# A layer of graph attention and routed low-rank feed-forward: the first pair of items on an uncentred W, with x centred instead

## The chip, the core and the metric

The program runs on one core of a Trainium2 chip. The core has five engines, each with its own queue of instructions carried out in order: TensorE (PE, matrix products), VectorE (DVE), ScalarE (ACT), GpSimd (POOL) and SyncE (SP, which here only issues transfers). They wait for each other through semaphores. Sixteen DMA engines move data between memory (HBM) and the core's SBUF; PE writes its results into PSUM. The metric is the time of one execution on the device in microseconds (us); less is better.

## The reference

The input x is 128 items of 128 rows by 1024 columns, adj a 128 x 128 matrix of 0 and 1 for each item. For each item:

```python
h  = layernorm(x)                       # over the 1024 columns, eps 1e-5
Wh = (h @ W) as 16 heads of 64          # W is 1024 x 1024
e  = leaky_relu(Wh . a1 + Wh . a2)      # one score per row and head
att = softmax(where(adj == 0, -9e15, e)) * adj
x1 = x + elu(att @ Wh)
n  = layernorm(x1)
gates = softmax of the top 2 of n[0] @ router.T   # 8 experts
x2 = x1 + n + sum over experts: gate * (n @ down.T) @ up
```

The score of a row does not depend on the column of adj, so softmax has two values per row. Two facts matter for the change. The mean that layernorm subtracts can be taken off x, or, since the same number is subtracted from a whole row of x, off the columns of W: (x - mean(x)) @ W = x @ (W - column mean of W) = (x - mean(x)) @ (W - column mean of W). And the score a . (x @ W) can be had from extra columns W . a ("score columns") that go through the same product.

## The kernel before

**Tiling.** Items are taken in pairs (q = 0 to 63), and pairs in groups of two (four items, g). For each pair the product with W is made by a Strassen-like scheme: x and W are cut into 2 x 2 blocks and seven block products take the place of eight. `pair_sums` (L245) makes the sums of the transposed x on POOL. `project` (L274) issues the seven products, `product_1` to `product_7`, each 8 fp32 matmuls (16 records in the trace) of 128 rows by 260 columns: 256 columns of W (`MAIN`) and 4 score columns (`SCORES`). W stands in SBUF as seven blocks of `w_sb`: B11, B21, B22, and the combinations T1, T2, T3, NT4; T1 first holds B12.

**Order.** The scheduler is off: each engine carries out its instructions in the order in which the code issues them. The loop at L692 has eight gaps for each pair; what stands in gap n is issued before the n-th product step. So the lists `gaps[...]` are the order of the work on every engine. In a pair's gaps stand: attention weights of the pair before (`attention_weights`, L368), `attend` and `update` of its two items, `second_stats`, `turn` (a 16-bit copy on ACT and a transposing DMA), `rejoin`, `join`, `high` and `low` (L358, L362: the product split into two parts for the attention matmuls), and the statistics (`first_stats`) and sums of the next pair. In the second pair of a group also `fetch`, `ffn_down`, `ffn_up` of the group before.

**Start.** SP and ACT load W in 16 pieces, then x_t of pair 0, adj, router and down matrices. `prepare` (L674) fills the gaps of pair 0. `spread_a` spreads a1 + a2 over the partitions, `column_means` (L153) makes the column means of W with 16 matmuls of 512 columns, `score_products` and `score_columns` (L161 to L179) make the score columns of all W on POOL and DVE, `center_block` (L188) subtracts the means from a block, score columns included, and `combine` (L671) and `weights_3_main` (L663) make the combinations. The block B11 is loaded, scored and centred before product_1 of pair 0.

**Experts.** `experts` (L195) centres the router and down matrices with 16 matmuls and two subtractions and stores the down rows as a table. It is issued ahead of pair 1's products.

Of the kernel before, what the change touches and what calls it, by code (L numbers as in the profile page):

```python
# [8 lines left out]
F32 = mybir.dt.float32  # L9
# [4 lines left out]
AF = mybir.ActivationFunctionType  # L14
# [11 lines left out]
def adj_ffn_kernel(  # L26
# [6 lines left out]
    w: bass.AP,  # L33
    a: bass.AP,
    down_t: bass.AP,
# [76 lines left out]
    a_rows = work.tile([1, 2, D], F32, tag="parts", name="a_rows", bufs=1)  # L112
    nc.sync.dma_start(a_rows, a[None])
    load_x(0)
    for h in range(NH):
        for k in range(KC):
            (nc.scalar, nc.sync)[k % 2].dma_start(
                w_at(h, k)[:, :, MAIN], in_two(w[k * P:(k + 1) * P, h * HALF:(h + 1) * HALF]))
    load_xt(0)
    router_sb = const.tile([P, KC, E], F32, name="router_sb")  # L120
    down_sb = work.tile([P, G * TOP, R, KC], F32, tag="down", name="down_sb", bufs=1)
    load_adj(0)
    nc.scalar.dma_start(router_sb, router_t)
    nc.scalar.dma_start(down_sb, down_t)
# [5 lines left out]
    one_row = const.tile([1, P], F32, name="one_row")  # L130
    nc.vector.memset(one_row, 1.0)
    mean_of = work.tile([P, P], F32, tag="dn", name="mean_of")
    nc.vector.memset(mean_of, 1.0 / D)
    ones_g = const.tile([G, P], F32, name="ones_g")
# [6 lines left out]
    a_sum = work.tile([P, NH, HALF], F32, tag="ex", name="a_sum", bufs=1)  # L141
    w_mean, score_mean = [], []

    def spread_a():

        nc.vector.tensor_add(a_rows[:, 0], a_rows[:, 0], a_rows[:, 1])
        for h in range(NH):
            pa = ps_m.tile([P, HALF], F32, tag="pm", name="pa")
            nc.tensor.matmul(pa, one_row, a_rows[:, 0, h * HALF:(h + 1) * HALF],
                             start=True, stop=True)  # L150
            nc.scalar.copy(a_sum[:, h], pa)

    def column_means(h):  # L153
        pc = ps_m.tile([P, HALF], F32, tag="pm", name="w_mean")
        for k in range(KC):
            nc.tensor.matmul(pc, mean_of, w_at(h, k)[:, :, MAIN], start=(k == 0),
                             stop=(k == KC - 1))
        w_mean.append(in_two(pc))


    def score_products(h):  # L161
        prod = work.tile([P, KC, 2, QC], F32, tag="y_t", name="prod", bufs=1)
        for k in range(KC):
            nc.gpsimd.tensor_tensor(prod[:, k], w_at(h, k)[:, :, MAIN], in_two(a_sum[:, h]),
                                    ALU.mult)
        return prod
# [4 lines left out]
    def score_columns(h, prod):  # L171
        for k in range(KC):
            by_head(w_at(h, k)[:, :, SCORES], prod[:, k])

    def score_columns_at_once(h):
        for k in range(KC):
            prod = work.tile([P, 2, QC], F32, tag="hp", name="prod")
            nc.vector.tensor_mul(prod, w_at(h, k)[:, :, MAIN], in_two(a_sum[:, h]))
            by_head(w_at(h, k)[:, :, SCORES], prod)  # L179

    def score_means(h):
        prod = work.tile([P, 2, QC], F32, tag="hp", name="prod")
        nc.vector.tensor_mul(prod, w_mean[h], in_two(a_sum[:, h]))
        mean = small.tile([P, 2, HPQ], F32, tag="score_mean", name="score_mean", bufs=2)
        by_head(mean, prod)
        score_mean.append(mean)

    def center_block(h, b):  # L188

        for cols, mean in ((MAIN, w_mean[h]), (SCORES, score_mean[h])):  # L190
            part = w_sb[:, b, :, :, cols]
            nc.vector.tensor_tensor(part, part, mean[:, None].to_broadcast(part.shape),
                                    ALU.subtract)

    def experts():  # L195

        pr = ps_m.tile([P, HALF], F32, tag="pm", name="pr")[:, 0:E]
        for k in range(KC):
            nc.tensor.matmul(pr, mean_of, router_sb[:, k], start=(k == 0), stop=(k == KC - 1))
        nc.vector.tensor_tensor(router_sb, router_sb,  # L200
                                pr[:, None].to_broadcast([P, KC, E]), ALU.subtract)
        pc = ps_m.tile([P, E, R], F32, tag="pm", name="pc")
        for k in range(KC):
            nc.tensor.matmul(pc, mean_of, down_sb[:, :, :, k], start=(k == 0), stop=(k == KC - 1))
        nc.vector.tensor_tensor(down_sb, down_sb,
                                pc[:, :, :, None].to_broadcast([P, E, R, KC]), ALU.subtract)
# [16 lines left out]
        return slot, down_row, up_row  # L223
# [50 lines left out]
    def project(q):  # L274
# [11 lines left out]

        def bank():
            return ps_w.tile([P, 2, HALF], F32, tag="pw", name="pw")

        def product(dst, first, lhs, rhs):  # L290
            for j in range(2):
                for k in range(KH):
                    nc.tensor.matmul(dst[:, j, 0:QE], lhs[:, k, :], w_sb[:, rhs, k, j],  # L293
# [6 lines left out]
        def read(dst, src, plus):  # L300
            nc.vector.tensor_tensor(dst, src[:, :, 0:QE], plus, ALU.add)  # L301

        p1, u2, u4 = (temp(n) for n in ("p1", "u2", "u4"))
        banks = {}
# [7 lines left out]
        def product_1():  # L312
            product(*to("x"), a11, B11)
            nc.scalar.copy(p1, banks["x"][:, :, 0:QE])

        def product_2():
            product(*to("x"), a12, B21)
            WH[q, 0] = banks["x"]
            high(q, 0)
# [475 lines left out]
```

## Time and profile before

Columns: what, time in us.

| | us |
|---|---|
| median of four runs | 1966.0 (1965.66 to 1968.01) |
| the profiled execution | 1966.55 |
| its span | 1963.6 |
| PE busy in the span | 1938.4 (99%) |
| DVE / ACT / POOL busy | 1664.7 / 1077.3 / 848.6 |
| first product of pair 0 starts on PE | 29.95 |
| first matmul of the experts | 61.36 |
| first product of pair 1 | 66.84 |
| product_4 of pair 1 | 89.75 |
| first logits (pair 2) | 116.44 |

Span is the time from the first to the last recorded instruction. An engine is busy while it carries out an instruction; waiting for a semaphore is not busy. fp32 matmuls appear as two records each. Gaps on PE are named with what ended them.

### The profile page before, as it was taken

How to read it: one execution, taken by the hardware profiler on the slowest of the kernel's cores; microseconds unless marked ns; L12 is line 12 of the kernel's file. 1: busy time of each engine (PE TensorE's matmuls, PEld its weight loads, DVE VectorE, ACT ScalarE, POOL GpSimd, SP SyncE). 2: the span in 40 equal slices, each digit the busy share in tenths (PEclk: the TensorE clock that was granted, in tenths of full speed). 3: DMA queues.
4: the chain of work that ended last, by engine and by line, in shares of the span. 5: the costliest groups of instructions: out<-in, count | busy, mean ns of one | idle time of the engine just before them, and what ended most of it. 6: DMA issues, size and time to landing. Idle time of an engine off the chain costs nothing.

```text
span 1963.6 us, 30104 instructions
## 1 busy us (share of the span) xinstructions
PE 1938.4 (99%) x11010; PEld 1577.0 (80%) x11010; DVE 1664.7 (85%) x3512; ACT 1077.3 (55%) x1027; POOL 848.6 (43%) x1128
## 2 busy tenths in 40 slices
PE   7999999999999999999999999999999999999997
PEld 4888888888888888888888888888888888888885
DVE  8788888888888888888888888898888898888886
ACT  0365555565555555555555655655655655655653
POOL 4353443553344553344543334544335544435530
PEclk9999999999999999999999999999999999999998
DMA  5356566555555565566565565565566565565552
GB/s 194 110 138 191 168 162 187 150 163 183 163 171 185 143 178 175 157 183 182 135 188 171 154 187 182 127 199 170 151 186 174 137 199 172 151 188 165 147 161 96
DMA packets 346580, 324.98 MB, mean 166 GB/s; under 512 B 274241, under 2 KB 280385, under 8 KB 346433
## 3 DMA queue, kind: packets, MB, share of 16 engines
q1 hardware_dynamic: 326386, 278.45, 48.8%
q0 software_dynamic: 17008, 40.91, 7.2%
q10 hardware_dynamic: 3040, 3.70, 0.6%
q8 instruction: 87, 1.43, 0.3%
q14 instruction: 59, 0.48, 0.1%
HBM read 189.31 MB, written 67.63 MB: 131 GB/s over the span
## 4 chain that ended last, share of the span: by engine, by line
PE 92%; DVE 4%; DMA 2%; ACT 1%; issue 0%; POOL 0%; ACTq 0%; DVEq 0%; POOLq 0%
PE pw L293 78%; PE ph L406 6%; PE pu L595 3%; PE pd L579 3%; PE pb L542 1%; DMA tt<-halves 1%; PE pl L486 1%; DMA w_sb<-in_w 1%; DVE xn L424 1%; DVE xn L425 1%; DVE hp L416 0%; DVE w_sb L169 0%; PE pu L656 0%; ACT halves L456 0%; ACT y_t L462 0%; DVE stats L229 0%
## 5 line engine op out<-in xcount | busy, mean ns | idle before, releaser
L293 PE MATMUL pw<-w_sb,xt 128*128 128x260 f32 x4096 | 947.5, 386 | 2.9 <-DVE parts L364 1.7
L293 PEld LDWEIGHTS pw<-w_sb,xt 128*128 128x128 f32 x4096 | 767.4, 190 | 149.2 <-issue 25.6
L293 PE MATMUL pw<-w_sb,s 128*128 128x260 f32 x3072 | 711.2, 385 | 3.3 <-DVE w_sb L672 2.5
L293 PEld LDWEIGHTS pw<-w_sb,s 128*128 128x128 f32 x3072 | 578.1, 190 | 116.4 <-issue 21.2
L233 POOL TENSOR_SCALAR rstd<-mv 128x2 f32<-128x2 f32 x128 | 29.1, 227 | 868.8 <-DVE mv L230 863.6
L462 ACT COPY y_t<-tt 128x2048 uint16<-128x2048 uint16 x126 | 312.8, 2502 | 67.5 <-DMA tt<-halves 67.3
L229 DVE BATCH_NORM_STATS2 stats<-xn 128x6 f32<-128x512 f32 x512 | 324.0, 675 | 5.4 <-DMA xn<-in_x 5.3
L560 POOL DMA_INDIRECT down<-table,at_down x248 | 251.7, 1015 | 162.3 <-DVE e L380 88.7
L456 ACT COPY halves<-xn 128x2048 uint16<-128x2048 uint16 x126 | 239.3, 1899 | 141.7 <-DVE xn L425 141.7
L360 ACT ACTIVATE parts<-wh,rstd 128x512 fp32r<-128x512 f32 x192 | 134.2, 716 | 235.7 <-DVE wh L301 235.7
L423 ACT ACTIVATE ex<-hp 128x1024 f32<-128x1024 f32 x128 | 135.4, 1058 | 178.8 <-DVE hp L416 178.8
L599 DVE SCALAR_TENSOR_TENSOR xn<-pu,rstd,xn 128x512 f32<-128x512 f32 x248 | 169.0, 744 | 21.8 <-PE pu L595 21.8
L416 DVE TENSOR_TENSOR hp<-ph,att 128x512 f32<-128x512 f32 x256 | 161.4, 672 | 9.9 <-PE ph L406 9.6
L425 DVE SCALAR_TENSOR_TENSOR xn<-ex,xn 128x1024 f32<-128x1024 f32 x128 | 156.9, 1226 | 14.0 <-DVE xn L424 0.9
L406 PE MATMUL ph<-parts,adj_f 128*128 128x512 f32 x512 | 164.3, 442 | 1.3 <-ACT parts L360 0.8
L301 DVE TENSOR_TENSOR wh<-pw,u 128x520 f32<-128x520 f32 x128 | 89.2, 697 | 84.7 <-PE pw L293 81.6
L424 DVE SCALAR_TENSOR_TENSOR xn<-hp,xn 128x1024 f32<-128x1024 f32 x128 | 156.8, 1225 | 4.4
L478 ACT ACTIVATE xn<-xn,off,mul 128x1024 f32<-128x1024 f32 x128 | 151.3, 1231 | 1.6 <-POOL off L443 1.6
L364 DVE SCALAR_TENSOR_TENSOR parts<-wh,rstd,parts 128x512 fp32r<-128x512 f32 x192 | 138.9, 751 | 12.0 <-ACT parts L360 12.0
L301 DVE TENSOR_TENSOR wh<-pw,p 128x520 f32<-128x520 f32 x64 | 44.8, 700 | 80.8 <-PE pw L293 80.8
L406 PEld LDWEIGHTS ph<-parts,adj_f 128*128 128x128 f32 x512 | 96.5, 189 | 20.3 <-ACT parts L360 1.2
L234 POOL TENSOR_TENSOR rstd<-rstd,half_pow 128x2 f32<-128x2 f32 x128 | 91.5, 715 | 10.6
(117 smaller groups left out, 1506.2 us busy)
## 6 DMA issues: line engine op xcount, KB each, us to landing
xn<-in_x SPq DMA_DIRECT2D x128, 512.0 KB, 6.8
xt<-in_x_t SPq DMA_DIRECT2D x128, 512.0 KB, 5.2
out_y<-xn SPq DMA_DIRECT2D x124, 512.0 KB, 3.9
adj_f<-in_adj_t POOLq DMA_DIRECT2D x32, 256.0 KB, 3.1
adj_i<-in_adj SPq DMA_DIRECT2D x32, 256.0 KB, 2.6
down<-table,at_down POOLq DMA_INDIRECT x248, 4.0
w_sb<-in_w ACTq DMA_DIRECT2D x8, 256.0 KB, 6.1
w_sb<-in_w SPq DMA_DIRECT2D x8, 256.0 KB, 5.6
```

Of the source, the lines that this page charges most:

```text
L229: nc.vector.bn_stats(st[:, h, :], X[i][:, h * HALF:(h + 1) * HALF])
L293: nc.tensor.matmul(dst[:, j, 0:QE], lhs[:, k, :], w_sb[:, rhs, k, j], start=(first and k == 0), stop=(k == KH - 1), skip_group_check=not f ...
L364: nc.vector.scalar_tensor_tensor(in_two(PARTS[q][:, 1, b]), block, rstd, in_two(PARTS[q][:, 0, b].bitcast(F32)), op0=ALU.mult, op1=ALU.sub ...
L406: nc.tensor.matmul(PH[i][h], GRP[g]["adj_f"][:, t, :], PARTS[q][:, s, NH * (i % 2) + h], start=(s == 0), stop=(s == 1))
L416: nc.vector.tensor_tensor(hp[:, h * HALF:(h + 1) * HALF].rearrange("p (h f) -> p h f", f=F), ph.rearrange("p (h f) -> p h f", f=F), att[:, ...
L424: nc.vector.scalar_tensor_tensor(xt, hp, 0.0, xt, op0=ALU.max, op1=ALU.add)
L425: nc.vector.scalar_tensor_tensor(xt, ex, 1.0, xt, op0=ALU.min, op1=ALU.add)
L456: nc.scalar.copy(halves, X[i].bitcast(U16).rearrange("p (d s) -> p s d", s=2))
L462: nc.scalar.copy(y_of(i).bitcast(U16).rearrange("p k (n s) -> p s k n", s=2), TT.pop(i).rearrange("p (s k) n -> p s k n", s=2))
L478: nc.scalar.activation(X[i], X[i], AF.Identity, bias=GRP[g]["off"][:, t:t + 1], scale=GRP[g]["mul"][:, t:t + 1])
L560: nc.gpsimd.indirect_dma_start(out=st["down"][:, j * R:(j + 1) * R].rearrange("p r k -> p (r k)"), out_offset=None, in_=table, in_offset=b ...
L599: nc.vector.scalar_tensor_tensor(y[:, cols], pu[t], st["rstd"][:, t:t + 1], y[:, cols], op0=ALU.mult, op1=ALU.add)
```

## The change

The first pair no longer needs a centred W. `center_x` subtracts the row means from the transposed x of pair 0, with means made on PE. product_1 and product_2 then use B11 and B21 as loaded. As product_1 alone covers half of the rows of W, its result p1 is corrected by `correct_p1` before the other products are added to it. B11, B21 and B22 are centred in place later, one after another, and T1, T2, T3 and NT4 are combined from them (T1 is no longer centred by itself).

The column means are made in two steps on PE column tiles: `partial_means` puts the sums of four k chunks into four strips of 32 partitions, and `column_means` adds the strips with one matmul. The score columns no longer come from products on POOL and DVE: a transposed copy of W (`w_t`) is loaded, `score_rows` multiplies it with a on column tiles, `center_rows` subtracts the mean, `turn_rows` transposes, and `score_columns` copies the results into `w_sb`. Pair 0 itself has products of 256 columns; its scores are made from its results by `score_of` (a product on POOL, a sum on DVE).

W is laid out on the host in four contiguous blocks. SP issues all loads: a, x_t, B11, B21, x, B22, T1 (B12), then W_t, adj, the next pair. The router and down matrices are loaded in gap 5 of pair 0, and `experts` now sums over the k chunks on DVE first, so that two matmuls do, and stands in gap 6 of pair 1, between product_3 and product_4. In pair 0, product_7 goes ahead of product_6, and the next pair's statistics and sums move from gaps 3 and 4 to gap 6.

```diff
-    for h in range(NH):
-        for k in range(KC):
-            (nc.scalar, nc.sync)[k % 2].dma_start(
-                w_at(h, k)[:, :, MAIN], in_two(w[k * P:(k + 1) * P, h * HALF:(h + 1) * HALF]))
     load_xt(0)
+    wt_sb = work.tile([P, KH, D], F32, tag="y_t", name="wt_sb", bufs=1)
+    wt_at = [wt_sb[:, c] for c in range(KH)]
+    wt_at += [work.tile([P, D], F32, tag="x", name="wt", bufs=10) for _ in range(KH)]
+    for i, b in enumerate((B11, B21, B22, T1)):
+        if i == 2:
+            load_x(0)
+        nc.sync.dma_start(w_sb[:, b], w[:, i])
+    nc.sync.dma_start(wt_sb, w_t[:, 0:KH])
+    for c in range(KH, KC):
+        nc.sync.dma_start(wt_at[c], w_t[:, c])
...
+    def center_x():
+        xt = XT[0]
+        px = ps_m.tile([P, HALF], F32, tag="pm", name="px")[:, 0:2 * P]
+        mean = px.rearrange("p (t n) -> p t n", t=2)
+        for k in range(KC):
+            nc.tensor.matmul(mean, mean_of, xt[:, :, k], start=(k == 0), stop=(k == KC - 1))
+        for t, lo, hi in ((0, 0, KH), (0, KH, KC), (1, 0, KC)):
+            part = xt[:, t, lo:hi]
+            nc.vector.tensor_tensor(part, part, mean[:, t, None].to_broadcast(part.shape),
+                                    ALU.subtract)
+
+    def partial_means(h):
+        pc = ps_m.tile([P, HALF], F32, tag="pm", name="pc")
+        for u in range(2):
+            for c in range(KH):
+                nc.tensor.matmul(pc[c * 32:(c + 1) * 32], mean_of[:, 0:32],
+                                 w_sb[:, BLOCK[h][u], c, :, MAIN], start=(u == 0), stop=(u == 1),
+                                 tile_position=(0, c * 32))
+        part = work.tile([P, HALF], F32, tag="hp", name="part")
+        nc.scalar.copy(part, pc)
+        return part
+
+    def column_means(part):
         pc = ps_m.tile([P, HALF], F32, tag="pm", name="w_mean")
-        for k in range(KC):
-            nc.tensor.matmul(pc, mean_of, w_at(h, k)[:, :, MAIN], start=(k == 0),
-                             stop=(k == KC - 1))
+        nc.tensor.matmul(pc, sum_of, part, start=True, stop=True)
         w_mean.append(in_two(pc))
...
+    def score_rows():
+        rows = [ps_m.tile([P, HALF], F32, tag="pm", name="rows") for _ in range(NH)]
+        for half in range(2):
+            for n in range(NH):
+                for t in range(KH):
+                    c = half * KH + t
+                    nc.tensor.matmul(rows[n][t * 32:(t + 1) * 32], a_two[:, c],
+                                     wt_at[c][:, n * HALF:(n + 1) * HALF],
+                                     start=(half == 0), stop=(half == 1),
+                                     tile_position=(0, t * 32))
+        return rows
+
+    def center_rows(rows):
+        sums = small.tile([P, NH], F32, tag="sums", name="sums", bufs=1)
+        for n in range(NH):
+            nc.vector.tensor_reduce(sums[:, n:n + 1], rows[n], AX.X, ALU.add)
...
+        for n in range(NH):
+            nc.scalar.activation(turned[:, n], rows[n], AF.Identity, bias=less)
+        return turned
+
+    def turn_rows(turned):
...
+            for k in range(KH):
+                nc.tensor.transpose(pt[:, k], turned[:, u, k * P:(k + 1) * P], ident)
...
+    def score_columns(cols):
...
+        for h, u, dst in ((0, 0, of[B11]), (0, 1, of[B21]), (1, 1, of[B22]), (1, 0, b12)):
+            src = cols[u].rearrange("p k (j t r) -> p k j t r", j=2, t=2)
+            for j in range(2):
+                nc.vector.tensor_copy(dst[:, :, j].rearrange("p k (t f) -> p k t f", t=2),
+                                      src[:, :, j, :, 2 * h:2 * h + 2])
+        nc.vector.tensor_tensor(of[T3], of[B22], b12, ALU.subtract)
+        for dst, x, y, op in ((T2, T3, B11, ALU.add), (T1, B22, T2, ALU.subtract),
+                              (NT4, B21, T2, ALU.subtract)):
+            nc.vector.tensor_tensor(of[dst], of[x], of[y], op)
+
+    def score_of(b):
...
+        nc.gpsimd.tensor_tensor(prod, src, a_sum[:, h], ALU.mult)
+        by_head(dst, prod)
...
     def experts():
-        pr = ps_m.tile([P, HALF], F32, tag="pm", name="pr")[:, 0:E]
-        for k in range(KC):
-            nc.tensor.matmul(pr, mean_of, router_sb[:, k], start=(k == 0), stop=(k == KC - 1))
...
+        for t, n in ((router_sb.rearrange("p k e -> p e k"), E), (down_rows, ER)):
+            sums = work.tile([P, ER], F32, tag="hp", name="sums")
+            nc.vector.tensor_reduce(sums[:, 0:n], t, AX.X, ALU.add)
+            pr = ps_m.tile([P, HALF], F32, tag="pm", name="pr")[:, 0:n]
+            nc.tensor.matmul(pr, mean_of, sums[:, 0:n], start=True, stop=True)
+            nc.vector.tensor_tensor(t, t, pr[:, :, None].to_broadcast([P, n, KC]), ALU.subtract)
...
+        gaps[0] += [(place_a,), (spread_a,), (center_x,), (pair_sums, 0)]
+        gaps[2] += [keep("part 0", partial_means, 0), (first_stats, 0),
+                    keep("less", first_half), (first_stats, 1),
+                    keep("", column_means, "part 0"), (keep_c11,), (high, 0, 0),
+                    (combine, T3, B22, T1, ALU.subtract)]
+        gaps[3] += [keep("part 1", partial_means, 1), (center_block, 0, B11),
+                    keep("", correct_p1, "less"), (combine, T2, T3, B11, ALU.add), (center_block, 0, B21)]
+        gaps[4] += [keep("", column_means, "part 1"), keep("rows", score_rows), (score_of, 0),
+                    (center_block, 1, B22), (combine, T1, B22, T2, ALU.subtract),
+                    keep("turned", center_rows, "rows")]
+        gaps[5] += [(combine, NT4, B21, T2, ALU.subtract), (load_experts,)]
+        gaps[6] += [keep("cols", turn_rows, "turned"), (score_of, 3)]
+        gaps[7] += [keep("", score_columns, "cols"), (score_of, 1)]
...
-            gaps[3].append((first_stats, 2 * q + 2))
-            gaps[4] += [(pair_sums, q + 1), (first_stats, 2 * q + 3)]
+            gaps[3 if q else 6].append((first_stats, 2 * q + 2))
+            gaps[4 if q else 6] += [(pair_sums, q + 1), (first_stats, 2 * q + 3)]
...
+        if q == 0:
+            gaps[7].append((score_of, 2))
         if q == 1:
-            slot, down_row, up_row = experts()
+            gaps[6].append((experts,))
```

## The prediction

> **What bounds the kernel now.** I read the engines' shares first, then the busy time by stretches, then the timeline of the first 120 us, the chain that ended last, and the groups of the operations that the change uses anew.
>
> ```profile
> PE 1938.4 (99%) x11010; PEld 1577.0 (80%) x11010; DVE 1664.7 (85%) x3512; ACT 1077.3 (55%) x1027; POOL 848.6 (43%) x1128
> 120.00:1900.00 1780.00, 1779.73 (x10278) 1458.15 (x10277) 1521.11 (x3254) 1013.43 (x963) 785.85 (x1050) 1.00 0.58 169
> ```
>
> The second line is a stretch: its length, then busy time of PE, its weight loads, DVE, ACT, POOL. From 120 us on PE is busy 1779.73 of 1780 us, and the change touches nothing there. So it is worth what it does to the moment at which PE reaches a fixed point of this stream; I take the last product of pair 1 (product_4), 89.75 us before.
>
> ```profile
> 29.95 3.77 PE L293 MATMUL pw<-w_sb,xt 128*128 128x260 f32 x16 [0.52 <-DVE w_sb L192]
> 40.70 3.77 PE L293 MATMUL pw<-w_sb,s 128*128 128x260 f32 x16 [2.52 <-DVE w_sb L672]
> 61.36 1.85 PE L199 MATMUL pr<-router_sb,mean_of 128*128 128x8 f32 x16
> 63.06 3.96 PE L204 MATMUL pc<-down_sb,mean_of 128*128 128x128 f32 x16
> 66.84 3.69 PE L293 MATMUL pw<-w_sb,xt 128*128 128x260 f32 x16
> 71.45 0.19 DVE L397 TENSOR_TENSOR att<-p,den 128x32 f32<-128x32 f32 x1
> ...
> 86.25 3.67 PE L293 MATMUL pw<-w_sb,s 128*128 128x260 f32 x16
> 89.75 7.18 PE L293 MATMUL pw<-w_sb,xt 128*128 128x260 f32 x32
> 92.42 1.32 ACT L360 ACTIVATE parts<-wh,rstd 128x512 fp32r<-128x512 f32 x2
> 93.16 1.42 DVE L364 SCALAR_TENSOR_TENSOR parts<-wh,rstd,parts 128x512 fp32r<-128x512 f32 x2 [2.50 <-ACT parts L360]
> ```
>
> Columns: start, length, engine, operation. Pair 0's products begin at 29.95, after W has been loaded, its score columns made and B11 centred; the experts' 32 matmul records hold PE from 61.36 to 66.84; pair 1 begins there. The last two lines matter most: pair 1's two low halves end at 94.57 (93.16 + 1.42), 4.8 us after product_3 of that pair left PE. No matmul before pair 1's attention waits for them now.
>
> ```profile
> 71.75 1.30 DVE hp L416 x2
> ...
> 81.50 1.91 ACT halves L456
> 83.43 4.31 DMA tt<-halves
> ...
> 90.15 2.36 ACT xn L478 x2
> 92.51 0.62 ACT parts L360
> 93.16 1.42 DVE parts L364 x2
> ```
>
> That is the chain (start, length) from attention's end at 71.64 to the lows: two updates on DVE, the 16-bit copy, the transposing DMA, rejoin, two joins, the highs. 22.93 us, of which PE sets nothing.
>
> **Gain in the head, step by step** (a sum of rows of the trace; columns per second of PE from rows: 16 records of 260 columns follow each other every 3.505 us, so 256 columns 3.45 us and 512 columns 0.43 us a record; 0.27 us more until the result is out, 3.77 less 3.50).
>
> Removed from ahead of the first product: on DVE eight score products and reduces (means 1.00 and 0.68 us), the score means and B11's centring, which fill 12.17 to 29.9; on PE 32 w_mean records; later the second reduces (4.8) and all centring of T1. SP takes over what ACT issued (10 transfers, some 0.5 us an issue, all gone out ahead of the data, which is 0.37 MB per us whatever the queue).
>
> x_t now goes first. In the trace 1.03 MB had moved by 5.42 us and then 0.37 MB per us; x_t and adj_f are 1.3 MB, so x_t is there at 6.5. Until 18.3 us PE ran at half pace (0.86 us between w_mean records, 0.43 after; 5.1 us after the 13.81 restart). center_x has 16 records of 256 columns: 12 at 0.43, 4 at 0.22, ending 12.7 with the drain. Bounds: full pace by 8 us, 1.5 earlier; half pace throughout, 1.2 later.
>
> Subtract 0.68, product_1 3.45 + 0.27, copy of p1 0.59, product_2 3.45: PE at 21.1. The loads of B11 and B21 (2.1 MB) are in by 12.5, so they hide. partial_means runs 16 records on four column tiles. The nearest row is the down product:
>
> ```profile
> L579 PE MATMUL pd<-y_t,down x1984: 272/273/328, 137.6 to 1915.7; 128*32 128x128 f32 x199
> 196.78 1.98 PE L579 MATMUL pd<-y_t,down 128*32 128x128 f32 x64
> ```
>
> 64 records of 128 columns in 1.9 us, 0.030 each: four tiles at once, so 0.119 for 512 columns and 1.9 us for sixteen. PE at 23.0, result 23.2; ACT copy 0.59; sum matmul 0.86; product_7 24.8 to 28.2, second partial_means to 30.1. T3 (DVE, 2.28) needs the last block of W: 6.4 MB, 19.5 us plus a landing, about 21; done 23.5, hidden under the DVE wait below.
>
> DVE: low of block 0 waits in order for its high (ACT: part copy, c11 copy 0.59, high 0.72, so 25.1) and ends 25.9; center B11 2.27, the p1 correction 0.75 (a 512-column row of this form), T2 2.28: 31.1; center B21 33.3. product_6 waits for T2 and starts 31.1, issues to 34.6; second sum matmul; score_rows 32 records, 3.8, to 39.3 (W_t, 4 MB more, is in by 33). DVE: u2 0.7 after product_6, a reduce 0.69, center B22, T1: 40.7. product_5 waits for it: 40.7 to 44.2. u4 0.7; product_3 45.2 to 48.6; eight transposes (the tail's 16 records took 2.1) 1.9; product_4 to 54.0, NT4 long ready at 48.1.
>
> Then PE waits. Pair 1's product_1 reads score columns that DVE writes in program order after: wh0 (50.1); score 3's reduce, whose product stands on POOL behind three mask operations (0.7) and adj_f's issue (0.68), so 52.2 and 52.9; two statistics 3.1; two lows 1.5; wh1 0.7; two copies. That is 58.2, against 66.84. The queue behind score 3's reduce is thus the price: some 4.2 us of PE. SP keeps up: its loads of x for pair 1 land by 38, and the experts' two loads are moved behind them and have 45 us.
>
> So pair 1 begins 8.6 us earlier. Of these 5.5 are the experts' matmuls, only moved; the pair itself ends 3 us earlier.
>
> **What is given back.** The experts now stand between product_3 and product_4 of pair 1. In PE's order the first matmul waits for a DVE reduce that stands behind the two lows. Attention of pair 0 ends late: POOL has pair 1's sums (rows of 5.24 together), rstd 0.94, and two score products 1.28 each, to 61.0; reduce 0.69; the 2.7 us from e to att: 64.4. Add the 22.93 of the chain: lows end 87.3. Reduce 0.22, matmul 0.48, the router subtraction 0.22, reduce of the down rows 1.22, second matmul: PE is free for product_4 at 89.8. product_3 had ended at 82.1 (58.2 + 22.9, and 1.0 for a DVE that runs 1.5 later against PE than before). PE thus waits 5.7 + 1.7 us there. Against 89.75: +0.1 us. Bounds from the chain: if the copy and rejoin rows vary as they do between pairs, 1.5 either way.
>
> **Pace of PE after the waits.** Ends: after 2.52 us of idle (before 40.70) the records kept their 381 ns, so 0; after 4.12 us (before 13.81) PE ran at half pace for 5.1 us, 2.55 lost, though it had not been at full pace ahead of that. I take 0 for the 4.2 us wait, since DVE and not PE sets what follows (0.7 at most), and for 5.7 + 1.7 a slow stretch that counts from the experts' first matmul, 2.0 us ahead of product_4: 3.1 us at half pace, 1.55 lost. Sum: 0.1 + 1.55 = +1.7.
>
> [...]
>
> The profiled run took 1966.55 us (span 1963.6 and 2.95 around it), 0.55 above the median of four, 1966.0. +1.7 makes 1968.3 for it, and **1967.7** for a median.
>
> **Rivals.**
> 1. Faster: the gain is kept. Place: the experts' wait in pair 1. If the chain from attention to the lows is shorter there than 22.93, or DVE reaches the experts' reduces soon after product_3 (wh0 0.7, highs and lows 1.5 to 3, then the two-matmul sequence 2.2), PE waits some 4.5 instead of 7.4 us and keeps its pace: 1962. For it speaks only that PE comes earlier; against it that ACT and the transposing DMA, not PE, end last in that chain.
> 2. Slower: the column tiles take turns. Place: 64 new records. At 0.43 us each instead of 0.119, the first partial_means costs 5.0 more, the second 4.0 (1.0 was waiting), score_rows 8.6 (1.4 was waiting): +17.6, 1985. It decides (crossing +3.9) from about 0.19 us a record. Against it stands the pd row, with four moving operands and weights reloaded as here.
> 3. Slower by pace: center_x at half pace throughout (+1.2), both waits followed by a slow stretch (+0.7 and 2.55): 0.1 + 4.5 = 1970.6. For it: the 13.81 row. Against: the first wait ends near the 4.12 us that is the shortest evidence.
> 4. It does not do what it says: a load of W or W_t is late. W_t has 6 us of cover under product_6, T1 2; beyond that each us costs one. Not likely at 0.37 MB per us.
>
> **How the numbers follow.** About 0.2%, 3.9 us, is what a measurement of this kernel can tell from no change. Forecast (head gain handed back, within 3.9): 0.60. Pace lost twice, or the chain late as well: 0.19. Tiles in turns or partly so: 0.07. Late load: 0.01. Gain kept: 0.13. Slower is 0.27, same 0.60, faster 0.13. The forecast's own bounds are 0.1 - 1.5 - 1.5 = 1963.1 and 0.1 + 1.5 + 1.2 + 2.55 + 0.7 = 1972; taking in the upper part of the faster rival, the range is 1962 to 1973.
>
> **What would show it.** Right: pair 1's first 260-column product near 58 us behind a wait of some 4 us for DVE; score_rows and partial_means at about 0.12 us a record; the experts' two matmuls near 88 and 89.5 with 5 to 6 and 1.7 us of idle before them, released by DVE reduces; product_4 of pair 1 within 3 us of 89.75; logits near 118 against 116.44; from there equal. Wrong: no wait at the experts, column-tile records at 0.4 us, or new idle after 120 us.

## The result and the profile after

The changed kernel takes 1970.45 us (median of 40 runs, 1968.76 to 1972.8), the kernel before, run beside it, 1967.35 (60 runs, 1965.16 to 1970.15). The ratio is 1.0016, with a 95% interval of 1.0011 to 1.0020: slower by 0.16%, some 3 us, which is inside the 0.2% that a measurement of this kernel can tell from no change. The four runs of before that were shown ahead of the prediction had a median 1.35 below that of the sixty.

The profiled execution of the changed kernel took 1970.55 us, span 1968.7; that of before 1966.55, 0.8 below its median of sixty. Comparisons of the two profiles so overstate the loss by some 0.9 us. First the engines' shares from the page after:

```profile
PE 1936.6 (98%) x11042; PEld 1576.0 (80%) x11042; DVE 1654.2 (84%) x3511; ACT 1080.8 (55%) x1031; POOL 837.2 (43%) x1123
```

and two stretches of it (length, then busy time of PE, of its weight loads (PEld), DVE, ACT, POOL, then the clock of PE that was granted, 1.00 being full speed, DMA share and GB/s):

```profile
120.00:1900.00 1780.00, 1779.48 (x10290) 1457.79 (x10290) 1520.17 (x3251) 1016.03 (x964) 788.32 (x1056) 1.00 0.58 169
60.00:125.00 65.00, 59.29 (x262) 49.63 (x260) 50.52 (x103) 32.64 (x30) 18.67 (x30) 0.91 0.32 83
```

From 120 us on PE is busy 1779.48 of 1780 us, against 1779.73 before: that part is as it was. Everything happens ahead of it, and in the second stretch (60 to 125 us) PE is idle for 5.7 us and its clock is 0.91. The timeline of PE after shows where (start, length, line, operation, and in brackets the idle time before it and what ended it):

```profile
50.14 3.62 PE L373 MATMUL pw<-w_sb,xt 128*128 128x256 f32 x16
59.34 2.94 PE L373 MATMUL pw<-w_sb,xt 128*128 128x260 f32 x6 [5.58 <-issue]
...
66.89 3.67 PE L373 MATMUL pw<-w_sb,s 128*128 128x260 f32 x16
...
81.84 3.67 PE L373 MATMUL pw<-w_sb,s 128*128 128x260 f32 x16
89.74 0.59 PE L283 MATMUL pr<-sums,mean_of 128*128 128x8 f32 x2 [4.23 <-DVE sums L281]
91.82 0.80 PE L283 MATMUL pr<-sums,mean_of 128*128 128x128 f32 x2 [1.48 <-DVE sums L281]
92.41 9.06 PE L373 MATMUL pw<-w_sb,xt 128*128 128x260 f32 x32
...
120.80 0.55 PE L568 MATMUL pl<-router_sb,y_t 128*4 128x8 f32 x16
```

Pair 0's last product is issued by 53.8, then PE waits 5.58 us. ("issue" means that the profile names no releaser. The products wait for the score columns: DVE's copies of them into `w_sb` start at 59.08.) Pair 1 begins at 59.34, 7.5 us earlier than before (66.84). It starts slowly: 6 records in 2.94 us, at half pace. product_3 of pair 1 starts at 81.84; then the experts' two matmuls wait 4.23 and 1.48 us for sums on DVE. product_4 of pair 1 and product_1 of pair 2, one row of 32 records, start at 92.41, 2.66 us later than before (89.75), and take 9.06 us where they took 7.18. The first logits come at 120.80, against 116.44. The head is 7.5 us shorter, and 60 us later PE is 4.4 us late.

The chain of waits after (start, length) says what carries that from pair 1's start on:

```profile
53.77 5.57 issue
59.34 6.79 PE pw L373 x16
...
76.51 1.91 ACT halves L538
...
78.43 4.26 DMA tt<-halves
...
85.09 2.36 ACT xn L560 x2
87.45 0.62 ACT parts L442
...
88.10 0.65 DVE parts L446
...
89.51 0.19 DVE sums L281
...
89.74 0.61 PE pr L283 x2
...
90.56 1.22 DVE sums L281
...
91.82 0.80 PE pr L283 x2
92.62 8.86 PE pw L373 x32
```

It is the chain shown for before, from the updates over the 16-bit copy, the transposing DMA and the highs to the lows on DVE (88.10 + 1.42 = 89.52), but with a new end: from the lows through the experts' sum, matmul, sum, matmul to product_4. Before, nothing of PE ahead of pair 1's attention hung on the lows. That the slow first product (59.34) stands on this chain does not make it dear: DVE's first update waited only 0.43 us for PE behind it, and experiment 5 puts a number to it.

### The profile page after: what moved, and what is told of

Read it like the earlier page. It is cut to its first block, busy times and chain, and to the rows that moved or that the text cites. A ratio compares the mean times of both kernels' runs of the same rounds, so it can differ in the third digit from the quotient of the medians.

```text
span 1968.7 us, 30167 instructions
## 1 busy us (share of the span) xinstructions
PE 1936.6 (98%) x11042; PEld 1576.0 (80%) x11042; DVE 1654.2 (84%) x3511; ACT 1080.8 (55%) x1031; POOL 837.2 (43%) x1123
## 4 chain that ended last, share of the span: by engine, by line
PE 92%; DVE 3%; DMA 2%; ACT 2%; issue 1%; POOL 0%; SPq 0%; POOLq 0%; DVEq 0%
PE pw L373 77%; PE ph L488 6%; PE pu L677 3%; PE pd L661 3%; DMA tt<-halves 1%; PE pb L624 1%; PE pl L568 1%; ACT y_t L544 1%; ACT halves L538 1%; DVE xn L507 1%; DVE xn L506 1%; DVE stats L306 0%; DVE hp L498 0%; PE pu L738 0%; DMA xt<-in_x_t 0%
## 5 line engine op out<-in xcount | busy, mean ns | idle before, releaser
L373 PE MATMUL pw<-w_sb,xt 128*128 128x260 f32 (+1 forms) x4096 | 952.3, 387 | 7.0 <-issue 5.6
L373 PE MATMUL pw<-w_sb,s 128*128 128x260 f32 (+1 forms) x3072 | 711.1, 385 | 2.9 <-DVE w_sb L746 2.0
L381 DVE TENSOR_TENSOR wh<-pw,u 128x520 f32<-128x520 f32 (+1 forms) x128 | 89.4, 698 | 88.4 <-PE pw L373 84.8
L381 DVE TENSOR_TENSOR wh<-pw,p 128x520 f32<-128x520 f32 (+1 forms) x64 | 44.8, 700 | 81.6 <-PE pw L373 81.6
L311 POOL TENSOR_TENSOR rstd<-rstd,half_pow 128x2 f32<-128x2 f32 x128 | 91.5, 715 | 10.6
```

Source lines behind the costliest of these rows:

```text
L373: nc.tensor.matmul(dst[:, j, cols], lhs[:, k, :], w_sb[:, rhs, k, j, cols], start=(first and k == 0), stop=(k == KH - 1), skip_group_check ...
```

## The experiments

The theory: the head's gain is real, and it is lost because the new `experts` stands between product_3 and product_4 of pair 1, behind the lows on DVE, which follow the end of pair 0's attention and not PE. The rivals: the loss comes from DVE's waits in pair 0 (score 3); it is the half clock after PE's idle times; or the new parts of the head, the column tiles above all, do not pay.

| | pair 1 starts | attention of pair 0 ends | first logits | median us | ratio to before, 95% |
|---|---|---|---|---|---|
| before | 66.84 | 71.64 | 116.44 | 1967.35 | 1 |
| the change | 59.34 | 66.19 | 120.80 | 1970.45 | 1.0016 (1.0011 to 1.0020) |
| experts as before | 59.58 | 68.34 | 114.13 | 1963.09 | 0.9975 (0.9965 to 0.9985) |
| experts' move alone | 62.9 | 67.40 | 121.62 | 1970.47 | 1.0011 (1.0002 to 1.0020) |
| score 3 later | 57.10 | 65.57 | 119.06 | 1969.04 | 1.0005 (0.9996 to 1.0014) |
| experts in two parts | 59.56 | 66.42 | 115.34 | 1965.11 | 0.9985 (0.9976 to 0.9994) |
| PE kept busy | 60.12 | 66.97 | 120.30 | 1969.07 | 1.0007 (0.9998 to 1.0016) |
| means without tiles | 68.72 | 75.58 | 129.98 | 1979.57 | 1.0061 (1.0047 to 1.0075) |
| experts as before, score 3 later | 59.68 | 67.92 | 113.04 | 1962.34 | 0.9976 (0.9965 to 0.9986) |
| lean experts | 58.77 | 65.09 | 114.92 | 1964.77 | 0.9986 (0.9977 to 0.9995) |
| lean experts, index rows first | 58.90 | 65.24 | 110.80 | 1960.16 | 0.9963 (0.9949 to 0.9976) |

The three times in the first columns are from each kernel's own profiled execution (attention's end is the end of the instruction `att`; 62.9 is 16 records after the 59.35 start of a row of 32). Logits and the profiled execution go together: from the logits to the span's end it is 1846 to 1848 us in all of them. Each ratio is to executions of the kernel before taken beside that kernel, whose medians lay between 1967.12 and 1968.26; across the rows the ratios are to be compared rather than the medians.

**1. Put the experts back.** The changed kernel, with the experts of before issued ahead of pair 1's products.

```diff
-            gaps[6].append((experts,))
+            slot, down_row, up_row = experts()   # 16 + 16 records on PE, no sums on DVE
```

> The changed kernel with the experts undone alone: 32 matmul records again, issued ahead of pair 1's products. Theory (the head's gain is handed back at the experts' wait between product_3 and product_4 of pair 1): PE waits 5.6 us before pair 1 in the changed kernel anyway and now spends it on the experts' 5.5 us, so pair 1 still begins near 59.5; product_4 follows product_3 at once, near 83 to 85 instead of 92.4; the logits come near 113 (120.8 in the changed kernel, 116.4 before): 3 us or 0.2% faster than before. Rival (the time is lost in pair 0, in DVE's wait or in the tiles): the logits stay near 120 and the time 3 us above before.

PE's timeline with the experts put back:

```profile
53.81 1.85 PE L277 MATMUL pr<-router_sb,mean_of 128*128 128x8 f32 x16
55.52 3.95 PE L282 MATMUL pc<-down_sb,mean_of 128*128 128x128 f32 x16
59.58 3.75 PE L374 MATMUL pw<-w_sb,xt 128*128 128x260 f32 x16
78.88 5.43 PE L374 MATMUL pw<-w_sb,xt 128*128 128x260 f32 x16 [2.11 <-issue]
87.65 7.18 PE L374 MATMUL pw<-w_sb,xt 128*128 128x260 f32 x32
```

The experts' 32 records fill the 5.6 us in which PE waited anyway, and pair 1 starts at 59.58 all the same: ahead of pair 1 they cost PE nothing in the changed kernel. They do cost DVE: with the subtractions ahead of it, attention of pair 0 ends at 68.34 instead of 66.19. product_4 starts at 87.65, 4.8 us sooner than with the change, and the time falls to 0.9975 of before. So the head's gain is real, and the experts, in place and form together, make the difference between -0.25% and +0.16%; experiment 4 keeps the new form and changes the place. A wait of 2.11 us remains in pair 1 and is followed by a slow product (5.43 instead of 3.67).

**2. The experts' move alone.** The kernel before, with only the new `experts` in gap 6 of pair 1.

```diff
-            slot, down_row, up_row = experts()
+            gaps[6].append((experts,))           # with the new experts()
```

> The kernel before with the new experts alone (DVE sums, two matmuls, between product_3 and product_4 of pair 1), head untouched. Theory: pair 1 begins 5.5 us earlier, near 61.4, but PE waits for the lows; DVE comes to attention some 6 us earlier, near 65.4, the lows end near 88.3, product_4 starts near 91 (89.75 before), and a slow stretch of PE adds up to 2: 1 to 3 us slower than before. Rival (the 32 records were the cost and the wait is hidden): 4 to 5 us faster.

PE's timeline with that move alone:

```profile
82.25 3.67 PE L292 MATMUL pw<-w_sb,s 128*128 128x260 f32 x16
90.83 0.59 PE L205 MATMUL pr<-sums,mean_of 128*128 128x8 f32 x2 [4.91 <-DVE sums L203]
92.91 0.80 PE L205 MATMUL pr<-sums,mean_of 128*128 128x128 f32 x2 [1.49 <-DVE sums L203]
93.50 8.71 PE L292 MATMUL pw<-w_sb,xt 128*128 128x260 f32 x32
```

The same two waits and the same slow stretch, without any of the new head. Pair 1 starts 4 us sooner and the kernel is 0.11% slower (1.0002 to 1.0020): this part of the change by itself gains nothing, and its loss, within the 0.2% of the measurement, is like that of the whole change. Of the 5.5 us that pair 1 should have gained, 1.5 were lost in pair 0 of this execution: the last 6 records of the product that ends at 45.97 took 2.35 us, where 7 took 1.70 before, and the next product starts at 47.70 instead of 46.20, both behind a wait of 1.72 us (see the last section).

**3. Score 3 later.** In the changed kernel the sum of score 3, which stood in DVE's queue ahead of pair 1's statistics and the lows, goes behind the score columns.

```diff
-        gaps[6] += [keep("cols", turn_rows, "turned"), (score_of, 3)]
-        gaps[7] += [keep("", score_columns, "cols"), (score_of, 1)]
+        gaps[6] += [keep("cols", turn_rows, "turned")]
+        gaps[7] += [keep("", score_columns, "cols"), (score_of, 3), (score_of, 1)]
```

> The changed kernel with the third score (POOL product and DVE sum) moved behind the score columns, so that DVE does not wait for it ahead of the statistics. Theory: pair 1 begins 2.5 to 3 us earlier (59.3 to about 56.5), but POOL's products end when they did, attention ends where it did (66.2) and the experts' matmuls and product_4 stay where they are (92.4 within 1): the time is that of the changed kernel, 3 us above before, within 1. Rival (DVE's wait in pair 0 sets the cost): 3 us faster than the changed kernel, level with before.

Pair 1 starts at 57.10, 2.2 us sooner; attention ends 0.6 us sooner, product_4 starts at 91.28 (1.1 sooner) behind waits of 5.26 and 1.49 us, and the time is within 0.1% of before. The expectation was the changed kernel's time within 1 us; by the ratios it is some 2 us better, which is nearer to what the rival said, though the two intervals overlap. The reading of the first wait (DVE behind score 3's sum, which waits for POOL) is right, but an earlier pair 1 mostly makes the experts' wait longer: 5.26 us instead of 4.23, with pair 1 2.2 us sooner and product_4 only 1.1. So score 3's place is at most a part of the loss: the ratio stays 0.3% above that of experiment 1, and with the experts back (experiment 7) moving score 3 changes nothing measurable.

**4. The experts in two parts.** Their two sums stay in gap 6 of pair 1; matmuls, subtractions and the rest go to gap 2 of pair 2.

```diff
-            gaps[6].append((experts,))
+            gaps[6].append((expert_sums,))
+        if q == 2:
+            gaps[2].append((experts,))
```

> The changed kernel with the experts' two DVE sums left in gap 6 of pair 1 and their two matmuls and the rest put into gap 2 of pair 2, where nothing waits. Theory: pair 1 begins near 59.3 as in the changed kernel, product_4 follows product_3 without a wait (near 85.6 instead of 92.4) and at full pace; 1 to 2 us come back as waits for a late DVE; logits near 113 to 114: 2 to 4 us faster than before. Rival (the loss sits in pair 0 or the pace): the time stays above before.

PE's timeline with the experts in two parts:

```profile
80.81 3.67 PE L381 MATMUL pw<-w_sb,s 128*128 128x260 f32 x16
84.32 7.18 PE L381 MATMUL pw<-w_sb,xt 128*128 128x260 f32 x32
...
96.68 0.60 PE L291 MATMUL pr<-sums,mean_of 128*128 128x8 f32 x4
...
106.47 5.43 PE L381 MATMUL pw<-w_sb,xt 128*128 128x260 f32 x16 [2.17 <-issue]
```

product_4 starts at 84.32 directly behind product_3, and the experts' records (96.68) wait for nothing. The head, the sums and the matmuls are those of the change; the place of the matmuls alone brings the ratio from 1.0016 to 0.9985, some 6 us by the ratios. 2 us are missing against the first experiment; a wait of 2.17 us has come up in pair 2 (before 106.47), again with a product of 5.43 us behind it, so that the logits come at 115.34 and not at the expected 113 to 114.

**5. Keep PE busy in the waits.** The changed kernel with 43 matmuls of ident by ident in the three waits (22, 16 and 5). Their results are used by nothing.

```diff
+    def filler(n):
+        pf = ps_m.tile([P, HALF], F32, tag="pm", name="pf")[:, 0:P]
+        for k in range(n):
+            nc.tensor.matmul(pf, ident, ident, start=(k == 0), stop=(k == n - 1))
...
+            if n > E:                             # in experts(), ahead of its second matmul
+                filler(5)
...
-            gaps[7].append((score_of, 2))
+            gaps[7] += [(score_of, 2), (filler, 22)]
...
-            gaps[6].append((experts,))
+            gaps[6] += [(filler, 16), (experts,)]
```

> The changed kernel with 43 matmuls of ident by ident (128 columns each, their result is used by nothing) put on PE into its three waits: 22 ahead of pair 1's first product, 16 ahead of the experts' first matmul, 5 between their two. They take PE's idle time and leave the waits' causes as they are. Theory (the slow stretches are TensorE's clock falling because PE had been idle, and the second one is paid in full): the granted clock stays near 1.00 from 55 to 125 us; product_1 of pair 1 takes 3.7 instead of 6.5 us; product_4 of pair 1 and product_1 of pair 2 together 7.2 instead of 9.06; the logits come near 118.5 instead of 120.8, and the time is some 2 us below the changed kernel's, within 0.1% of before. Rival (the pace is no cost, what was lost there comes back in later waits): logits at 120.8 and the time as the changed kernel's.

PE's timeline with PE kept busy:

```profile
54.37 5.07 PE L278 MATMUL pf<-ident 128*128 128x128 f32 x44
60.12 3.75 PE L382 MATMUL pw<-w_sb,xt 128*128 128x260 f32 x16 [0.67 <-PE pf L278]
...
84.60 3.73 PE L278 MATMUL pf<-ident 128*128 128x128 f32 x32
90.28 0.39 PE L292 MATMUL pr<-sums,mean_of 128*128 128x8 f32 x2 [1.96 <-DVE sums L288]
...
92.75 8.23 PE L382 MATMUL pw<-w_sb,xt 128*128 128x260 f32 x32
```

Pair 1's first product keeps its pace (3.75 us instead of 6.79), so its slow start was the idle PE. But it brings little: this run was 0.78 us late already at product_2 of pair 0 (19.04 against 18.26), attention ends 0.78 late, and the experts' first sum, at 89.97 against 89.43, comes only 0.24 us sooner once that is taken off. The slow start is thus nearly all off the path, since DVE sets the second wait; 0.24 us is no more than that stretch of the chain varies between the kernels here (22.8 to 23.3 us). The second slow stretch is on the path; the filler covers half of it (8.23 us, between 7.18 and 9.06): the clock still fell, at about 91.5, behind the 1.96 us of idle that were left. The gain is 1.4 us between the medians and 1.8 by the ratios, where 2 had been expected, with intervals of the two ratios that overlap; the logits came at 120.30, not near 118.5. The pace is thus at most a part of the loss: the ratio stays 0.3% above that of experiment 1. Against the small loss of 0.16% either this or experiment 3 looks large; against the 0.4% that the experts make, both are small.

**6. The column means without tiles.** The changed kernel, with 8 matmuls of the full array for each half of W, as before, in place of `partial_means` and the sum.

```diff
-        nc.tensor.matmul(pc, sum_of, part, start=True, stop=True)
+        for k in range(KC):
+            nc.tensor.matmul(pc, mean_of, w_at(h, k)[:, :, MAIN], start=(k == 0),
+                             stop=(k == KC - 1))
```

> The changed kernel with the column tiles undone for the column means alone: each half of W has 8 matmuls of the full array with 512 columns, as before, in place of partial_means, the copy and the sum matmul. Theory (four column tiles work at once, 0.12 us a record): each of the two means takes 6.9 us of PE instead of some 2 + 0.6 + 0.9, product_7 starts some 3.5 us later, the rest of pair 0 some 4 to 7 us later, pair 1 near 63 to 66 instead of 59.3, logits near 124 to 127; the time is 4 to 8 us above the changed kernel's. Rival (the tiles save nothing on the path, DVE's centring sets pair 0's end anyway): pair 1 within 1 us of 59.3 and the time as the changed kernel's.

Each of the two now is 16 records in 7.03 us, 0.43 us a record; on tiles the same columns took 1.93 us, and the first 16 records of `score_rows`, from 36.03 to the next row at 37.78, 0.11 a record. Pair 1 starts 9.4 us later than with the change; 1.1 of that was there at product_2 already, a variation between runs, and some 8.3 are the tiles: +3.2 ahead of product_7, -0.6 ahead of product_6, +5.7 ahead of product_5. The time is 1.0061 of before, 9 us above the change; 4 to 8 had been expected. The loss arrives nearly in full at the logits (129.98, 9.2 later), since attention ends 9.4 later as well. The tiles pay, and at 0.11 against 0.43 us a record the rival that they take turns is out.

**7. and 8. Better places for the experts.** Experiment 1 with score 3 later, and "lean" experts: their 32 records ahead of pair 1, their means copied by ACT, both subtractions on POOL in gap 4 of pair 1, the index rows in gap 3 of pair 2, and score 3 later.

```diff
+        if q == 1:
+            expert_means()                        # 16 + 16 records, two copies on ACT
+            gaps[4].append((expert_subtract,))    # POOL
+        if q == 2:
+            gaps[3].append((experts,))            # table and index rows
```

> The changed kernel with the experts put back ahead of pair 1 as they were before, and score 3 moved from gap 6 to gap 7 of pair 0. Theory (PE's time ahead of pair 1 is filled by the experts' 32 records, so that score 3 no longer sets pair 1's start): pair 1 at 59 to 59.6 as with the experts alone put back, logits within 1 us of 114.1, the time within 0.1% of 1963.1. Rival (DVE's order there still costs: lows and attention come earlier once score 3 is out of their way): attention ends 1 to 2 us earlier than 68.2, the waits in pair 1 shrink, logits 1 to 2 us earlier.

> The changed kernel with the experts put back ahead of pair 1 as matmuls only (16 + 16 records in PE's wait there), their means copied to SBUF by ACT, both subtractions on POOL in gap 4 of pair 1, the index rows in gap 3 of pair 2, and score 3 moved one gap later. So the experts cost neither PE nor DVE anything that is waited for. Theory (what the change gained in the head is kept once nothing of the experts stands on DVE ahead of attention): pair 1 starts at 58 to 59.5, attention ends near 65.5 against 68.2 with the experts as before, no wait of more than 1.5 us on PE after that, logits near 111 to 113 and the time 1 to 3 us below that of the kernel with the experts as before (1963.1). Rival (POOL's subtractions delay the sums or attention by as much as DVE is relieved): logits near 114 and no difference from it.

With the experts as before, score 3 later changes nothing that can be measured (0.9976 against 0.9975); attention ends 0.4 us sooner, and the logits come 1.1 sooner in the profile because the product behind the wait of 2.11 us kept its pace this time (3.75 instead of 5.43); 0.94 us of that went into a wait for ACT ahead of the logits. The lean experts did what was expected of attention (65.09, 3.2 sooner than in experiment 1) and were still slower than experiment 1 (0.9986 against 0.9975) instead of 1 to 3 us faster. PE and DVE with the lean experts:

```profile
104.86 0.23 DVE L303 TENSOR_REDUCE slot<-ident 128x8 f32<-128x128 f32 x1
108.09 0.33 DVE L308 TENSOR_TENSOR at_r<-rows,ident 128x128 f32<-128x128 int32 x1 [3.00 <-DMA tt<-halves]
109.56 5.43 PE L387 MATMUL pw<-w_sb,s 128*128 128x260 f32 x16 [3.61 <-DVE u L395]
```

The index rows stood in a place where their buffer (one of those that the code calls `hp`, which the 16-bit copy `halves` uses too) was still being read by a transposing DMA. DVE waited 3.00 us, PE behind it 3.61, and its next product ran slowly.

**9. The index rows first.** The same, with the index rows made at the very start.

```diff
+    index_rows()
     for q in range(NQ + 2):
```

> The kernel with the lean experts (matmuls ahead of pair 1, subtractions on POOL in pair 1, score 3 one gap later), with one thing more: the index rows of the experts are made at the very start, while DVE and POOL wait for x_t, and no longer in gap 3 of pair 2. There their second instruction on DVE stood 3.0 us behind a transposing DMA that was still reading the buffer it takes over, product_3 of pair 2 came 3.61 us late, and it ran slowly (5.43 instead of 3.67 us). Theory (that wait alone hid what the lean experts bring): attention of pair 0 ends near 65.1 as there, no wait of more than 1 us on PE between 58.8 and the logits, logits at 114.9 - 3.6 - 1.8 = 109.5, some 3.5 us before the 113.0 of the kernel with the experts as before and score 3 later; the time 1959 us, 0.4% below before. Rival (the order on DVE and ACT then waits somewhere else): a new wait of 2 us or more in pair 1 or 2, logits at 112 or later, time 1962 or more.

PE's timeline with the index rows first:

```profile
53.42 1.85 PE L279 MATMUL pr<-router_sb,mean_of 128*128 128x8 f32 x16
58.90 3.69 PE L387 MATMUL pw<-w_sb,xt 128*128 128x260 f32 x16
75.78 3.74 PE L387 MATMUL pw<-w_sb,xt 128*128 128x260 f32 x16 [0.81 <-issue]
82.86 7.18 PE L387 MATMUL pw<-w_sb,xt 128*128 128x260 f32 x32
110.80 0.55 PE L582 MATMUL pl<-router_sb,y_t 128*4 128x8 f32 x16 [1.17 <-ACT y_t L558]
```

No wait above 1.2 us is left between 53 us and the logits. The time is 1960.16, 0.9963 of before (0.9949 to 0.9976): 7 us faster than before and 10 faster than the change. 1959 and logits at 109.5 had been expected; the logits come at 110.80, 1.17 of it a wait for ACT's copy, which no term of that sum held.

## Why the prediction was right

It said 1967.7 us, same, with the head's gain given back at the experts: 1970.45 came, ratio 1.0016. The mechanism was the forecast's, shown by experiments 1 and 4, and experiment 2 agrees. The number is 2.75 us off: 1.35 of that lie in the kernel before, whose four executions had a median of 1966.0 where sixty had 1967.35, and 1.4 in the sum. Point by point:

- **Head to product_4 of pair 0.** 54.0 predicted, 53.77 measured. x_t came at 7.9 instead of 6.5 and product_7 started at 25.50 instead of 24.8; product_6 at 31.55 (31.1), product_5 at 41.14 (40.7), product_3 at 45.74 (45.2). Column tiles: 1.93 and 1.92 us for 16 records of 512 columns, 1.9 predicted from a row of another operation; transposes 1.04 instead of 1.9.
- **First wait.** 4.2 predicted, 5.58 measured; pair 1 at 59.34 instead of 58.2. The sum of score 3 ended at 53.3 (52.9). Missing is 1.0 us on the two lows, 2.54 instead of 1.5: the second of them, at 56.81, took 1.75 us beside a sum of 1.71 us on POOL (56.30), where a low at 88.77, with POOL idle, took 0.75.
- **Attention.** 64.4 predicted, 66.19 measured; the 2.7 us from the scores to its end were right (63.52 to 66.19). POOL's two score products ended at 61.92 instead of 61.0, and the prediction put one sum of 0.69 us directly behind them. In fact both sums stood on DVE behind four small instructions that took 2.43 us, and ran from 62.22 to 63.49. This 1.8 us is the largest single miss of the sum.
- **The experts' two waits.** 5.7 and 1.7 us with the matmuls near 88 and 89.5 predicted; 4.23 and 1.48 measured, at 89.74 and 91.82. (By the prediction's own terms, 87.3 + 0.22 against 82.1, the first would have been 5.4.) The wait was shorter because product_3 left PE at 85.51 and not at 82.1: pair 1 began 1.1 late and its first product lost 3.1 us at half pace. Since DVE's chain and not PE sets its end, this moved no later event.
- **The chain to the lows.** 22.93 predicted from the row before; 23.33 measured, and 22.8 to 23.3 in every other kernel run here. From the lows' end to product_4 2.89 instead of 2.5.
- **product_4 of pair 1.** +0.1 predicted against before, +2.66 measured: 1.8 + 0.4 + 0.4.
- **Pace.** 1.55 predicted behind the experts' wait, 1.88 measured (9.06 - 7.18). For the first wait 0 was taken: there was a slow stretch that cost PE 3.1 us, but on the path it made at most some 0.24 us, as experiment 5 shows. So 0 was right for the reason that it gave (DVE sets what follows), not because PE kept its pace.
- **Sum.** +1.7 predicted; +4.4 at the logits of the profiles, +3.1 between the medians. The forecast was low because attention of pair 0 ended 1.8 us late in a place where the sum had not counted what DVE's instructions cost beside POOL (2.43 us for four small ones that take 0.71 with score 3 later). The bounds (1.5 us on the chain) were given to the wrong term, the copies and the rejoin, which hardly varied.
- **Rivals.** "Gain kept" named the right point (DVE reaching the experts' sums soon after product_3); it did not happen, and experiments 1 and 9 are that case brought about by hand. "Column tiles in turns" and "a late load" did not happen. "Pace lost twice" came near in its time (1970.6), but by chance: its second loss was there, the first was off the path. Two small slips change nothing: the price of "gain kept" comes to some 1963.2 by its own terms (2.9 us less wait and no 1.55) and not to 1962, and in the kernel before the half pace behind 13.81 lasted to 18.9 (13.81 + 5.1), not to 18.3.

## What to carry to other kernels

An engine that starts earlier gains nothing at a point which hangs on another engine's chain. Here the time of the logits is attention's end plus 45 us in four kernels (before 44.8, experts as before 45.8 and, with score 3 later, 45.1, index rows first 45.6) and plus 53.3 to 54.6 in the five that have the experts' sums and matmuls behind the lows; the two others, each with one wait of its own in pair 2, lie between (two parts 48.9, lean 49.8). So look for the chain's start, and put new work where an engine waits anyway, not behind the end of that chain. Price small instructions at what they cost beside the other engine that will be running then (here 2.43 us instead of 0.71 for four on DVE, beside POOL), and before moving one ask which buffer it takes over and who still reads it.

## What the runs showed of the hardware

**DVE held up by POOL.** DVE's instructions of the score columns, and POOL's second product, in the changed kernel:

```profile
59.84 0.91 DVE L256 TENSOR_TENSOR w_sb<-w_sb,b 128x32 f32<-128x32 f32 x1
60.78 1.19 DVE L259 TENSOR_TENSOR w_sb<-w_sb 128x32 f32<-128x32 f32 x1
62.01 0.29 DVE L259 TENSOR_TENSOR w_sb<-w_sb 128x32 f32<-128x32 f32 x2
60.65 1.27 POOL L270 TENSOR_TENSOR prod<-wh,a_sum 128x512 f32<-128x512 f32 x1
```

The first one ends at 60.75, as POOL's first product does (59.43 + 1.28 = 60.71); the second at 61.97, as POOL's second does (61.92); the next two, with POOL idle, take 0.29 together. With score 3 later the same four end at 58.35, ahead of POOL's products (DVE waits for the first of those until 59.71), and take 0.19 and 0.52 us. By these ends the two long ones did not run at a lower rate: each stood until POOL's was over. DVE's copies at 59.57 took 0.24 us beside POOL's first product, as they do with score 3 later (57.33); which instructions are held up, and why, is not shown beyond these rows.

**When the clock falls.** By the granted clock in short stretches, PE was at 0.50 from 58.7 to 65.5 and from 89.4 to 96.2 in the changed kernel, 6.8 us each; it fell during idle times of 5.6 and 4.2 us, shortly before PE started again. With the experts as before it fell at 80.1, 1.2 us after PE had started again from only 2.11 us of idle, and came back at 83.5. With score 3 later as well, the same 2.11 us of idle left it at 1.00. So did 2.52 us in the kernel before, ahead of 40.70 (3.77 us for that product), while in experiment 2, whose pair 0 is the same, that product's last records ran slowly (2.35 us for 6) and the mean clock of the first 60 us was 0.97, against 1.00 before. The stretch behind the wait of 2.11 us with the experts as before:

```profile
80.00:83.40 3.40, 3.40 (x9) 2.66 (x9) 3.33 (x8) 2.49 (x2) 2.76 (x7) 0.51 0.68 130
```

and with score 3 later as well:

```profile
78.50:82.00 3.50, 3.50 (x16) 3.02 (x17) 3.43 (x8) 3.50 (x2) 1.87 (x6) 1.00 0.34 66
```

9 records of PE in 3.40 us at a clock of 0.51 there, 16 in 3.50 at 1.00 here. A wait of some 2 us was thus a gamble for 1.8 us here (5.43 - 3.67); each one of over 4 us between 50 and 105 us was followed by a slow product that took 1.2 to 3.1 us more. The clock stayed down for 3.4 us with the experts as before and for 6.8 us twice in the changed kernel, and it fell after idle times of 1.96, 2.11 and 2.17 us (experiments 5, 1 and 4), but not after the 2.11 and 2.52 us above. Which idle time is enough stays open: no run here was made for it.
